# Weight sums, product order, bias and stores in a routed-LoRA FFN kernel

## The chip, the core and the metric

The kernel runs on one core of a Trainium2 chip. A core has TensorE (PE), VectorE (DVE), ScalarE (ACT), GpSimd (POOL) and SyncE (SP, which here only issues DMAs); each runs its own instructions in order, and they meet through semaphores. The metric is the device time of one execution in microseconds.

## The reference, cut to what matters

```python
z = einsum('bct,bcd->bdt', x, W[condition])        # 64 samples, 64x64 matrix for each, T = 1024
logits = einsum('bsd,ed->bse', z, gate_w)           # 8 experts, two are kept, softmax over the two
low    = einsum('bsd,erd->ebsr', z, lora_A)         # rank 16 for each expert
ffn    = z @ base_w.T + base_b + 2.0 * (low weighted by the gate) @ lora_B
out    = x + ffn
```

There are 64 x 64 = 4096 tokens of 1024 values, in fp32.

## The kernel before, in words

The per-sample 64x64 mix and the large product commute, so the kernel first multiplies x by all weights (lora_A, gate and base, 1160 columns) and then mixes tokens with a block-diagonal matrix (`bdr`, gathered for each tile by an indirect DMA on POOL). Every fp32 operand is split into a high part (a cast, mostly ACT, L199) and a low part (a subtraction, mostly DVE, L196), and each product is three matmuls: high x high, high x low, low x high.

The tokens are 32 tiles of 128. The 1160 columns are two halves of 580, each cut into chunks of 344 and 236 columns (`CS`), so that a tile has chunks c = 0 to 3. The contraction of 1024 is two halves of four k-blocks of 128. A product result goes to a PSUM bank z0 to z3; `split_z` splits it, and `sums` (L316) multiplies it by the block-diagonal matrix, adds the LoRA part, and leaves it in a bank a or o; `finish` (L334, DVE) adds that to the token tile `xtok`, which holds x and the bias; `store` (L339) writes the tile out. Chunk 0 also gives the gate (L344), whose small operations lead to a transpose (`tr`) and then to the LoRA matmuls.

Tiles 0 to 3 are done plainly (the first pair and the second, `plain`, L475). From tile 4 on, two tiles are taken as a 2x2 block product with seven products instead of eight (`pair`, L537): p1, p6, p2, p7, q4, q5, q3. Their weights are b11, b21 and b22, which are parts of the weight matrix, and t1 to t4, which are sums of parts; `sum_w` (L251) makes the sums in four rounds, each with four loads into the staging tiles `st`, four sums on DVE and four splits, while the second plain pair runs. The x operands are sums as well (`sum_x`, L230). The pairs use the staging tiles for their combinations u, v and w (L544 to L550).

The order of instructions on each engine is worked out by a list planner (`Program`, L55 to L134): each step has engines, an estimated cost, what it reads and writes, a due time and a lag, the time between a step's end and its result being there. A step goes to the engine that can begin first; at equal readiness the one with the earliest latest start goes first. Loads without inputs are held back until 10 us (`AHEAD`) before that. The real engines then run in that order and wait where the real times are longer. SP issues all plain loads and all stores; POOL issues the gathers and a few early splits.

Buffers that matter here: six raw x tiles (`xr`), three token tiles (tile i uses i % 3), four staging tiles, two block-diagonal tiles. Each token tile is loaded by `load_tok` (L268), and DVE adds the bias, which lies broadcast in `bias_bc`:

```python
add(SP, 1.45, lambda e: nc.sync.dma_start(xtok[j], x[i * P:(i + 1) * P, :]), ...)
add(DVE, 1.2, lambda e: nc.vector.tensor_tensor(xtok[j], xtok[j], bias_bc, ALU.add), ...)
```

Of the kernel before, what the change touches and what calls it, by code (L numbers as in the profile page):

```python
# [20 lines left out]
P = 128  # L21
# [22 lines left out]
SAME = {PE: 0.0, ACT: 0.1, DVE: 0.12, POOL: 0.1, SP: 1.0}  # L44
START = {PE: 0.0, ACT: 2.0, DVE: 0.8, POOL: 1.7, SP: 1.6}
GATHER = 8.0
AHEAD = 10.0
MARGIN = 1.2
COL = 0.0004557
LEAST = 0.107  # L50
PAIR = 28.6
LAG, LAST = 16.0, 8.0


# [83 lines left out]
def cond_ffn_kernel(ctx, tc, xT, x, idx, cw, wall, bias, lb, out):  # L138
# [15 lines left out]
    def many(n, shape, dt, name):  # L154
        return [sb.tile(shape, dt, name=f"{name}{j}") for j in range(n)]
# [4 lines left out]
    wl = {(m, s): sb.tile([P, KH, n], F32R, name=f"wl_{m}_{s}") for m in NAMES for s, n in enumerate(CS)}  # L160
    BLOCK = (("b11", "t4"), ("b21", "b22"))
    lbh, lbl = sb.tile([P, T], F32R, name="lbh"), sb.tile([P, T], F32R, name="lbl")
    bias_bc = sb.tile([P, T], F32, name="bias_bc")
    ident = sb.tile([P, P], F32, name="ident")
    NXR, NXA, NZ = 6, 4, 3
    xr, xtok = many(NXR, [P, KH, P], F32, "xr"), many(3, [P, T], F32, "xtok")
    xh, xl = many(NXA, [P, KH, P], F32R, "xh"), many(NXA, [P, KH, P], F32R, "xl")
    st = many(4, [P, 2 * CS[0]], F32, "st")
    bdr, bdh, bdl = many(2, [P, P], F32, "bdr"), many(2, [P, P], F32R, "bdh"), many(2, [P, P], F32R, "bdl")
    zh, zl = many(NZ, [P, CS[0]], F32R, "zh"), many(NZ, [P, CS[0]], F32R, "zl")  # L170
    low = many(2, [P, NG + 6], F32, "low")
# [23 lines left out]
    def sub(e, o, a, b):  # L195
        eng[e].tensor_tensor(o, a, b.bitcast(F32), ALU.subtract)  # L196
# [8 lines left out]
        return turns[kind] % n  # L205

    def tt_cost(n, e=DVE):
        return 0.08 + 0.00104 * n if e == DVE else 0.12 + 0.0022 * n


    def load_x(i, h, pieces=1):

        j, n = take("xr", NXR), KH // pieces
        for k in range(0, KH, n):
            add(SP, 0.182 * n, lambda e, k=k: nc.sync.dma_start(xr[j][:, k:k + n], xT[i][:, KH * h + k:KH * h + k + n]),  # L215
                writes=[("xr", j, q) for q in range(k, k + n)])
        return j

    def split_x(r, pieces=1, hi=ACT, lo=DVE):
# [10 lines left out]
    def sum_x(o, a, b, f):  # L230
        keys = lambda r: [("xr", r, q) for q in range(KH)]
        add(DVE, tt_cost(P * KH), lambda e: nc.vector.tensor_tensor(xr[o], xr[a], xr[b], f),  # L232
            [k for r in (a, b) if r != o for k in keys(r)], keys(o))


    def piece(j, s):
        return st[j][:, :2 * CS[s]].rearrange("p (k n) -> p k n", k=2)
# [5 lines left out]
    def split_w(j, m, s, k, hi=ACT, lo=DVE):  # L243
        n, a, q = 2 * CS[s], slice(k, k + 2), range(k, k + 2)
        src = [("st", j, 0), ("st", j, 1)]
        add(hi, 0.2 + (0.00083 if hi == ACT else 0.00052) * n, lambda e: copy(e, wh[m, s][:, a], piece(j, s)),
            src, [("wh", m, s, b) for b in q])
        add(lo, tt_cost(n, lo), lambda e: sub(e, wl[m, s][:, a], piece(j, s), wh[m, s][:, a]),
            src + [("wh", m, s, b) for b in q], [("wl", m, s, b) for b in q])

    def sum_w(s, k):  # L251
        keys = lambda j: [("st", j, 0), ("st", j, 1)]

        def plus(o, a, b):
            add(DVE, tt_cost(2 * CS[s]), lambda e: nc.vector.tensor_tensor(piece(o, s), piece(a, s), piece(b, s), ALU.add),  # L255
                keys(b if o == a else a), keys(o))
        for j, (h, n) in enumerate(((0, 0), (0, 1), (1, 1), (1, 0))):
            load_w(j, h, n, s, k)
        plus(0, 0, 1)
        split_w(0, "t1", s, k)  # L260
        plus(1, 1, 2)
        split_w(1, "t3", s, k)
        plus(0, 0, 2)
        split_w(0, "t2", s, k)
        plus(3, 3, 0)
        split_w(3, "t4", s, k)

    def load_tok(i):  # L268
        j = i % 3
        add(SP, 1.45, lambda e: nc.sync.dma_start(xtok[j], x[i * P:(i + 1) * P, :]),  # L270
            writes=[("xtok", j, c) for c in range(4)])
        add(DVE, 1.2, lambda e: nc.vector.tensor_tensor(xtok[j], xtok[j], bias_bc, ALU.add),  # L272
            ["bias"], [("xtok", j, c) for c in range(4)])

    def load_cond(i):

# [9 lines left out]
    due = {}  # L286

    def mm_cost(n):
        return max(COL * n, LEAST)

    def zstep(key, b, a, ka, m, s, start, stop):

# [45 lines left out]

    def store(i, cs):  # L339
        o, j = slice(outs(cs[0])[1].start, outs(cs[-1])[1].stop), i % 3  # L340
        add(SP, 0.00145 * (o.stop - o.start),
            lambda e: nc.sync.dma_start(out[i * P:(i + 1) * P, o], xtok[j][:, o]), [("xtok", j, c) for c in cs])

    def gate(i, b):  # L344

# [53 lines left out]

    ORDER = [(i, 0, k) for k in range(KT) for i in range(2)]  # L400
    ORDER += [(i, c, k) for i, c in ((0, 1), (1, 1), (0, 2), (0, 3), (1, 2), (1, 3)) for k in range(KT)]
    PRODUCTS = ("p1", "p6", "p2", "p7", "q4", "q5", "q3")
    t = 4.2
    for i, c, k in ORDER:
# [3 lines left out]
    for q in range(1, NPLAIN):  # L408
        for i in (2 * q, 2 * q + 1):
            for c in range(4):  # L410
                for k in range(KT):
                    due["plain", i, c, k] = t
                    t += 3 * mm_cost(CS[c % 2]) * 1.27
        ends.append(t)
    for q in range(NPLAIN, NPAIR):
        for p in PRODUCTS:
            for s in range(2):
                for k in range(KH):
                    due[q, p, s, k] = t
                    t += PAIR / 56 * 2 * CS[s] / HALF  # L420
        ends.append(t)
# [13 lines left out]
    def load_split_x(i, h, **engines):  # L435
        raw0[i, h] = load_x(i, h, 2)
        xa0[i, h] = split_x(raw0[i, h], 2, **engines)

    def first_loads():
        for h in range(2):  # L440
            for i in range(2):
                load_split_x(i, h, lo=POOL)
                load_split_w(h, 0, 0, 2 * i)
    first_loads()

# [15 lines left out]
    for s in range(2):  # L461
        for h in range(2):
            for k in range(0, KH, 2):
                load_split_w(h, 1, s, k)
    add(SP, 1.45, lambda e: nc.sync.dma_start(bias_bc, bias.broadcast_to([P, T])), writes=["bias"])
    load_tok(0)
    lraw = [("xtok", 2, c) for c in range(4)]
    add(SP, 1.45, lambda e: nc.sync.dma_start(xtok[2], lb), writes=lraw)
# [41 lines left out]
    def operands(q):  # L510

        a, b = 2 * q, 2 * q + 1
        a11 = load_x(a, 0)
        yield split_x(a11)
        a21, a22 = load_x(b, 0), load_x(b, 1)
        s3 = take("xr", NXR)
        sum_x(s3, a11, a21, ALU.subtract)
        sum_x(a21, a21, a22, ALU.subtract)
        sum_x(a11, a21, a11, ALU.subtract)
        yield split_x(a11)  # L520
        a12 = load_x(a, 1)
        yield split_x(a12)
        yield split_x(s3)
        yield split_x(a22)
        yield split_x(a21)
        sum_x(a12, a12, a11, ALU.add)
        yield split_x(a12)
# [9 lines left out]
    def pair(q):  # L537
        a, b = 2 * q, 2 * q + 1
        bx, by = (("z0", "z1"), ("z2", "z3"))[::1 if q % 2 else -1]
        u, v, w = q % 2, 2, 3  # L540
        part = lambda j, s: st[j][:, s * CS[0]:s * CS[0] + CS[s]]
        z = lambda bs, s: bank[bs[s]][:, :CS[s]]

        def combine(o, x, y, f, bs, reads=()):  # L544

            def then(s):
                at = {"o": part(o, s), "u": part(u, s), "v": part(v, s), "z": z(bs, s)}
                add(DVE, 0.09 + 0.00104 * CS[s], lambda e: nc.vector.tensor_tensor(at["o"], at[x], at[y], f),  # L548
                    [bs[s]] + [("st", j, s) for j in reads if j != o], [("st", o, s)])
            return then  # L550

        def chunk(i, n, o):
            return lambda s: post(i, 2 * n + s, split_z(CS[s], part(o, s), ("st", o, s), 0.05))

        ops = operands(q)
        product(q, "p1", next(ops), bx, True, False, lambda s: add(
            ACT, 0.2 + 0.00085 * CS[s], lambda e: copy(e, part(u, s), z(bx, s)), [bx[s]], [("st", u, s)]))
        product(q, "p6", next(ops), by, True, True, combine(u, "u", "z", ALU.add, by))
        product(q, "p2", next(ops), bx, False, True,
                lambda s: post(a, s, split_z(CS[s], z(bx, s), bx[s])))  # L560
        product(q, "p7", next(ops), by, True, False, combine(v, "u", "z", ALU.add, by, (u,)))

        def both(f, g):
            return lambda s: (f(s), g(s))
        product(q, "q4", next(ops), by, False, True,
                both(combine(w, "u", "z", ALU.add, by, (u,)), chunk(b, 0, w)))
        product(q, "q5", next(ops), bx, True, False,
                both(combine(v, "z", "v", ALU.subtract, bx), chunk(b, 1, v)))
        store(b, range(4))
        product(q, "q3", next(ops), bx, False, True,  # L570
                both(combine(u, "z", "u", ALU.subtract, bx), chunk(a, 1, u)))
        if q < NPAIR - 1:
            store(a, range(4))
        else:
            for cs in ((0, 1), (2,), (3,)):
                store(a, cs)
# [48 lines left out]
```

## Time and profile before

| | us |
|---|---|
| median of 3 runs | 507.07 (505.77 to 507.86) |
| the profiled execution | 507.96 |
| its span, first to last instruction | 506.1 |
| first matmul of the product / last matmul of all, start | 4.80 / 501.95 |
| mean granted TensorE clock | 0.990 |
| DMA share in 0-50 / 60-95 / 95-490 | 0.73 / 0.42 / 0.33 |

The page gives the busy time and share of each engine, then the span in 40 slices, the DMA queues, the chain of work that ended last, groups of instructions, and DMA issues. A group is named by line, engine, operation and out<-in tiles. A wait is given as "who <- whom: us in total, times, longest". In rows in order of time, the first number is the start and the second the duration, both in us; "[1.0 <-DVE st L548]" is idle time before it and what ended it. A line can be that of a helper: L196 is every subtraction of a split and L199 every cast.

### The profile page before, as it was taken

Reading aid. Unit: us, or ns where it says so; the run is one execution under the profiler, and the core shown is the slowest. Engines: PE = TensorE matmul, PEld = TensorE weight load, DVE = VectorE, ACT = ScalarE, POOL = GpSimd, SP = SyncE. Lnnn points to the kernel's source line nnn. Section 1 sums busy time; section 2 is a strip of 40 time slices with the busy share of each in tenths; the row PEclk is TensorE's granted clock in tenths of the full one; section 3 lists DMA queues with packets and bytes.
Section 4 is the critical chain, followed back from the end, with each engine's and each line's share of the span. In section 5 each row is a group of like instructions: output and inputs, shape, how many; then the busy total and the mean of one; then the engine's idle time right before and its main releaser. Section 6 shows DMA issues by size and latency. Waiting matters only on the chain.

```text
span 506.1 us, 9262 instructions
## 1 busy us (share of the span) xinstructions
PE 484.9 (96%) x3565; PEld 479.0 (95%) x3565; DVE 370.9 (73%) x959; ACT 175.3 (35%) x429; POOL 44.1 (9%) x49
## 2 busy tenths in 40 slices
PE   8999985999999999999999999999999999999996
PEld 7989975999999999999999998999999999999996
DVE  3768679786876858778686876858687686867765
ACT  6634335233332323333142332324242232423312
POOL 6310000010100001010010101001020100101000
PEclk8999999899999999999999999999999999999999
DMA  8884635142508043070704316061340606134042
GB/s 253 279 310 125 207 98 162 43 155 74 188 2 272 10 148 112 6 230 6 248 13 136 126 41 214 7 202 59 110 153 38 213 12 208 53 120 141 2 166 84
DMA packets 25292, 63.60 MB, mean 126 GB/s; under 512 B 3216, under 2 KB 6688, under 8 KB 25248
## 3 DMA queue, kind: packets, MB, share of 16 engines
q1 hardware_dynamic: 24192, 60.89, 35.7%
q0 software_dynamic: 1056, 2.12, 1.4%
q8 instruction: 28, 0.46, 0.4%
q14 instruction: 16, 0.13, 0.1%
HBM read 46.22 MB, written 16.78 MB: 124 GB/s over the span
## 4 chain that ended last, share of the span: by engine, by line
PE 73%; DMA 14%; DVE 8%; issue 1%; ACT 1%; SPq 1%; DVEq 0%; ACTq 0%
PE ps_z L298 56%; PE ps_o L329 12%; DMA xr<-in_xT 8%; DMA st<-in_w 6%; PE ps_a L329 4%; DVE st L255 1%; DVE wl_t L196 1%; DVE xl L196 1%; DVE xtok L336 1%; DVE wl_b L196 1%; DVE st L548 1%; DVE xr L232 1%; PE ps_a L372 1%; DVE zl L196 1%; SPq L215 1%
## 5 line engine op out<-in xcount | busy, mean ns | idle before, releaser
L298 PE MATMUL ps_z<-wh_t,xh 128*128 128x344 f32 x480 | 145.3, 303 | 9.3 <-DVE st L548 5.2
L298 PE MATMUL ps_z<-wl_t,xh 128*128 128x344 f32 x480 | 143.1, 298 | 1.0 <-DVE wl_t L196 1.0
L298 PE MATMUL ps_z<-wh_t,xl 128*128 128x344 f32 x480 | 142.8, 297 | 0.0
L298 PE MATMUL ps_z<-wh_b,xh 128*128 128x344 f32 (+1 forms) x432 | 131.9, 305 | 3.1 <-DVE zl L196 2.4
L298 PE MATMUL ps_z<-wl_b,xh 128*128 128x344 f32 (+1 forms) x432 | 130.3, 302 | 0.4 <-DVE wl_b L196 0.4
L298 PE MATMUL ps_z<-wh_b,xl 128*128 128x344 f32 (+1 forms) x432 | 129.8, 301 | 0.4 <-POOL xl L196 0.4
L298 PEld LDWEIGHTS ps_z<-wh_t,xh 128*128 128x128 f32 x480 | 91.1, 190 | 11.7 <-DVE st L548 6.9
L298 PEld LDWEIGHTS ps_z<-wl_t,xh 128*128 128x128 f32 x480 | 91.2, 190 | 1.5 <-DVE wl_t L196 1.5
L298 PEld LDWEIGHTS ps_z<-wh_t,xl 128*128 128x128 f32 x480 | 91.1, 190 | 0.0
L199 ACT CAST xh<-xr 128x512 fp32r<-128x512 f32 (+1 forms) x110 | 66.2, 605 | 70.2 <-PE ps_z L298 57.7
L298 PEld LDWEIGHTS ps_z<-wh_b,xh 128*128 128x128 f32 x432 | 83.2, 193 | 4.3 <-DVE zl L196 2.9
L298 PEld LDWEIGHTS ps_z<-wl_b,xh 128*128 128x128 f32 x432 | 83.2, 193 | 0.9 <-DVE wl_b L196 0.9
L298 PEld LDWEIGHTS ps_z<-wh_b,xl 128*128 128x128 f32 x432 | 83.1, 192 | 0.9 <-POOL xl L196 0.9
L196 DVE TENSOR_TENSOR xl<-xr,xh 128x512 fp32r<-128x512 f32 x102 | 69.8, 685 | 5.0 <-ACT xh L199 3.9
L278 POOL DMA_INDIRECT bdr<-in_cw,rows x32 | 33.7, 1053 | 414.2 <-DVE bdl L196 385.8
L199 ACT CAST zh<-st 128x344 fp32r<-128x344 f32 (+1 forms) x84 | 36.6, 436 | 83.7 <-DVE st L548 41.4
L336 DVE TENSOR_TENSOR xtok<-ps_o,xtok 128x344 f32<-128x344 f32 (+1 forms) x96 | 42.1, 439 | 32.0 <-PE ps_o L329 31.5
L232 DVE TENSOR_TENSOR xr<-xr,xr 128x512 f32<-128x512 f32 x56 | 38.5, 687 | 20.2 <-DMA xr<-in_xT 20.0
L548 DVE TENSOR_TENSOR st<-st,ps_z 128x344 f32<-128x344 f32 x84 | 37.6, 450 | 11.5 <-PE ps_z L298 11.3
L272 DVE TENSOR_TENSOR xtok<-xtok,bias_bc 128x1024 f32<-128x1024 f32 x32 | 38.8, 1214 | 7.9 <-DMA xtok<-in_x 7.9
L199 ACT CAST zh<-ps_z 128x344 fp32r<-128x344 f32 (+1 forms) x44 | 17.6, 400 | 69.7 <-PE ps_z L298 52.7
L196 DVE TENSOR_TENSOR zl<-st,zh 128x344 fp32r<-128x344 f32 (+1 forms) x84 | 37.9, 454 | 0.9
(68 smaller groups left out, 626.8 us busy)
## 6 DMA issues: line engine op xcount, KB each, us to landing
xtok<-in_x SPq DMA_DIRECT2D x32, 512.0 KB, 6.0
out<-xtok SPq DMA_DIRECT2D x31, 512.0 KB, 2.9
xr<-in_xT SPq DMA_DIRECT2D x60, 256.0 KB, 4.5
st<-in_w SPq DMA_DIRECT2D x16, 344.0 KB, 4.5
st<-in_w SPq DMA_DIRECT2D x16, 236.0 KB, 2.9
xr<-in_xT SPq DMA_DIRECT2D x8, 128.0 KB, 4.7
bdr<-in_cw,rows POOLq DMA_INDIRECT x32, 2.5
xtok<-in_lb SPq DMA_DIRECT2D x1, 512.0 KB, 5.7
```

The source lines that it names most:

```text
L196: eng[e].tensor_tensor(o, a, b.bitcast(F32), ALU.subtract)
L199: (nc.scalar.copy if e == ACT else nc.vector.tensor_copy)(o, a)
L215: add(SP, 0.182 * n, lambda e, k=k: nc.sync.dma_start(xr[j][:, k:k + n], xT[i][:, KH * h + k:KH * h + k + n]), writes=[("xr", j, q) for q ...
L232: add(DVE, tt_cost(P * KH), lambda e: nc.vector.tensor_tensor(xr[o], xr[a], xr[b], f), [k for r in (a, b) if r != o for k in keys(r)], key ...
L255: add(DVE, tt_cost(2 * CS[s]), lambda e: nc.vector.tensor_tensor(piece(o, s), piece(a, s), piece(b, s), ALU.add), keys(b if o == a else a) ...
L272: add(DVE, 1.2, lambda e: nc.vector.tensor_tensor(xtok[j], xtok[j], bias_bc, ALU.add), ["bias"], [("xtok", j, c) for c in range(4)])
L278: add(POOL, 1.04, lambda e: nc.gpsimd.indirect_dma_start(out=bdr[j], out_offset=None, in_=cw, in_offset=bass.IndirectOffsetOnAxis(ap=rows[ ...
L298: nc.tensor.matmul(z, l[a][:, ka, :], w[m, s][:, ka, :], start=(start and q == 0), stop=(stop and q == 2), skip_group_check=True)
L329: nc.tensor.matmul(d, l, r, start=(start and m == 0), stop=(stop and m == len(mms) - 1), skip_group_check=True)
L336: add(DVE, 0.09 + 0.00104 * (s.stop - s.start), lambda e: nc.vector.tensor_tensor(xtok[j][:, o], bank[b][:, s], xtok[j][:, o], ALU.add), [ ...
L372: add(PE, 0.107, lambda e: nc.tensor.matmul(tp, low[i % 2][:, :ER], ident, is_transpose=True, start=False, stop=False, skip_group_check=True),
L548: add(DVE, 0.09 + 0.00104 * CS[s], lambda e: nc.vector.tensor_tensor(at["o"], at[x], at[y], f), [bs[s]] + [("st", j, s) for j in reads if ...
```

## The change

- `sum_w`: the four sums are made first, in place (st0 = b00 + b01 for t1, st1 = st1 + st2 for t3, st2 = st2 + st0 for t2, st3 = st3 + st2 for t4); then the splits follow in the order t2, t3, t4, t1, and their low parts may go to DVE or POOL.
- The first pair (`NPLAIN`) runs its products in the order p1, p2, q3, p6, p7, q4, q5, with its own bank use, operand order and an additional staging tile; both stores come at its end.
- The bias tile goes. After the token load a DMA issued by POOL adds the bias, read broadcast from HBM, into the token tile.
- The stores of all but the last two tiles are issued by POOL.
- `xr` has seven buffers, `st` five. The low parts of the first x operand go to DVE instead of POOL.
- The planner gets lags for x loads (2.0), token loads (4.0), the accumulating DMA (5.0) and POOL's stores (2.0), and other costs for matmuls and POOL.

```diff
-COL = 0.0004557
-LEAST = 0.107
-PAIR = 28.6
+XLAG = 2.0
+COL, SET = 0.000418, 0.014
+LEAST = 0.111
+PAIR = 29.1
...
-    bias_bc = sb.tile([P, T], F32, name="bias_bc")
-    NXR, NXA, NZ = 6, 4, 3
+    NXR, NXA, NZ = 7, 4, 3
-    st = many(4, [P, 2 * CS[0]], F32, "st")
+    st = many(5, [P, 2 * CS[0]], F32, "st")
...
-        return 0.08 + 0.00104 * n if e == DVE else 0.12 + 0.0022 * n
+        return 0.08 + 0.00104 * n if e == DVE else 0.15 + 0.0035 * n
...
-                writes=[("xr", j, q) for q in range(k, k + n)])
+                writes=[("xr", j, q) for q in range(k, k + n)], lag=XLAG if pieces == 1 else 0.0)
...
         plus(0, 0, 1)
-        split_w(0, "t1", s, k)
         plus(1, 1, 2)
-        split_w(1, "t3", s, k)
-        plus(0, 0, 2)
-        split_w(0, "t2", s, k)
-        plus(3, 3, 0)
-        split_w(3, "t4", s, k)
+        plus(2, 2, 0)
+        plus(3, 3, 2)
+        for j, m in ((2, "t2"), (1, "t3"), (3, "t4"), (0, "t1")):
+            split_w(j, m, s, k, lo=(DVE, POOL))
...
-        add(SP, 1.45, lambda e: nc.sync.dma_start(xtok[j], x[i * P:(i + 1) * P, :]),
-            writes=[("xtok", j, c) for c in range(4)])
-        add(DVE, 1.2, lambda e: nc.vector.tensor_tensor(xtok[j], xtok[j], bias_bc, ALU.add),
-            ["bias"], [("xtok", j, c) for c in range(4)])
+        keys = [("xtok", j, c) for c in range(4)]
+        add(SP, 1.45, lambda e: nc.sync.dma_start(xtok[j], x[i * P:(i + 1) * P, :]), writes=keys, lag=4.0)
+        add(POOL, 1.1, lambda e: nc.gpsimd.dma_start(xtok[j], bias.broadcast_to([P, T]), accum_op=ALU.add),
+            writes=keys, lag=5.0)
...
-        return max(COL * n, LEAST)
+        return max(COL * n + SET, LEAST)
...
-        add(SP, 0.00145 * (o.stop - o.start),
-            lambda e: nc.sync.dma_start(out[i * P:(i + 1) * P, o], xtok[j][:, o]), [("xtok", j, c) for c in cs])
+        src = [("xtok", j, c) for c in cs]
+        if i < NT - 2:
+            add(POOL, 1.0, lambda e: nc.gpsimd.dma_start(out[i * P:(i + 1) * P, o], xtok[j][:, o]), src, lag=2.0)
+        else:
+            add(SP, 0.5, lambda e: nc.sync.dma_start(out[i * P:(i + 1) * P, o], xtok[j][:, o]), src)
...
+    FIRST = ("p1", "p2", "q3", "p6", "p7", "q4", "q5")
...
-                    t += 3 * mm_cost(CS[c % 2]) * 1.27
+                    t += 3 * mm_cost(CS[c % 2]) * 1.25
-        for p in PRODUCTS:
+        for p in FIRST if q == NPLAIN else PRODUCTS:
...
-                load_split_x(i, h, lo=POOL)
+                load_split_x(i, h, lo=POOL if h or i else DVE)
...
-    add(SP, 1.45, lambda e: nc.sync.dma_start(bias_bc, bias.broadcast_to([P, T])), writes=["bias"])
...
         yield split_x(a11)
+        if q == NPLAIN:
+            a12 = load_x(a, 1)
+            yield split_x(a12)
...
+        if q == NPLAIN:
+            sum_x(a12, a12, a11, ALU.add)
+            for r in (a12, a11, s3, a22, a21):
+                yield split_x(r)
+            return
...
-        u, v, w = q % 2, 2, 3
+        u, v, w = 4 if q == NPLAIN else q % 2, 2, 3
...
+        if q == NPLAIN:
+
+            t = 1
+            product(q, "p2", next(ops), bx, False, True,
+                    lambda s: post(a, s, split_z(CS[s], z(bx, s), bx[s])))
+            product(q, "q3", next(ops), by, True, True, lambda s: None)
+            product(q, "p6", next(ops), bx, True, True,
+                    both(combine(u, "u", "z", ALU.add, bx), combine(t, "y", "u", ALU.subtract, by, (u,))))
+            product(q, "p7", next(ops), bx, True, False, combine(v, "u", "z", ALU.add, bx, (u,)))
+            product(q, "q4", next(ops), bx, False, True,
+                    both(combine(w, "u", "z", ALU.add, bx, (u,)), chunk(b, 0, w)))
+            product(q, "q5", next(ops), by, True, True,
+                    both(both(combine(v, "z", "v", ALU.subtract, by), chunk(b, 1, v)),
+                         both(combine(t, "z", "t", ALU.add, by), chunk(a, 1, t))))
+            store(b, range(4))
+            store(a, range(4))
+            return
```

More of the change, by code (lines that the diff above doesn't have):

```diff
@@ L247, in split_w @@
             src, [("wh", m, s, b) for b in q])
-        add(lo, tt_cost(n, lo), lambda e: sub(e, wl[m, s][:, a], piece(j, s), wh[m, s][:, a]),
+        lo = lo if isinstance(lo, tuple) else (lo,)
+        add(lo, [tt_cost(n, e) for e in lo], lambda e: sub(e, wl[m, s][:, a], piece(j, s), wh[m, s][:, a]),
             src + [("wh", m, s, b) for b in q], [("wl", m, s, b) for b in q])
@@ L255, in plus @@
             add(DVE, tt_cost(2 * CS[s]), lambda e: nc.vector.tensor_tensor(piece(o, s), piece(a, s), piece(b, s), ALU.add),
-                keys(b if o == a else a), keys(o))
+                [q for j in (a, b) if j != o for q in keys(j)], keys(o))
         for j, (h, n) in enumerate(((0, 0), (0, 1), (1, 1), (1, 0))):
@@ L546, in then @@
             def then(s):
-                at = {"o": part(o, s), "u": part(u, s), "v": part(v, s), "z": z(bs, s)}
+                at = {"o": part(o, s), "u": part(u, s), "v": part(v, s), "t": part(1, s), "z": z(bs, s)}
+                at["y"] = at["z"]
                 add(DVE, 0.09 + 0.00104 * CS[s], lambda e: nc.vector.tensor_tensor(at["o"], at[x], at[y], f),
@@ L553, in chunk, with both @@
             return lambda s: post(i, 2 * n + s, split_z(CS[s], part(o, s), ("st", o, s), 0.05))
+        def both(f, g):
+            return lambda s: (f(s), g(s))
         ops = operands(q)
@@ L561, in pair @@
         product(q, "p7", next(ops), by, True, False, combine(v, "u", "z", ALU.add, by, (u,)))
-        def both(f, g):
-            return lambda s: (f(s), g(s))
         product(q, "q4", next(ops), by, False, True,
```

## The prediction

> **What bounds the kernel now.** I read the page's busy times first, then stretches of the span, then the matmul rows, and only then asked who is waited for. TensorE is busy or queued nearly always:
>
> ```profile
> PE 484.9 (96%) x3565; PEld 479.0 (95%) x3565; DVE 370.9 (73%) x959; ACT 175.3 (35%) x429; POOL 44.1 (9%) x49
> ...
> PEclk8999999899999999999999999999999999999999
> ```
>
> In the rows in order of time, back-to-back matmuls start 0.1575 us apart at 344 columns, 0.1115 at 236 and 0.107 at 208, so the matmul work has a price that no edit here changes. A plain tile is 8 x 3 x 2 x (0.1575 + 0.1115) = 12.9 us, a pair's seven products 7 x 12 x 0.269 = 22.6; the sums of one tile are 3.2. Four plain tiles (64.4) and 14 pairs (29.0 each, 405.4) make 469.8. The first real matmul starts at 4.80 and the last at 501.95: 497.2 us, so **27.3 us are lost**. Adding up, row by row, what each start is later than its spacing gives 6.5 us lost in 0-50, 0.0 in 50-60, 11.4 in 60-95, 8.4 in 95-490 and 1.1 after. The stretches (length, then busy time and instructions of each engine, granted clock, DMA) show the same place:
>
> ```profile
> 50.00:60.00 10.00, 10.00 (x74) 10.00 (x73) 7.10 (x16) 3.50 (x8) 0.94 (x1) 1.00 0.64 199
> 60.00:95.00 35.00, 27.27 (x182) 26.45 (x181) 26.02 (x57) 13.21 (x28) 1.15 (x1) 0.90 0.42 133
> 95.00:490.00 395.00, 389.85 (x2911) 387.73 (x2910) 295.69 (x789) 130.83 (x333) 27.33 (x26) 1.00 0.33 111
> ```
>
> So there are two things to gain: a bad 35 us while the weight sums are made, and a small repeated loss in the pairs. In the first, three stalls carry it: 1.7 us at 62.87, 2.0 at 74.62, and 7.5 from 82.49 to 92. The third, in TensorE's rows:
>
> ```profile
> 82.49 0.27 PE L298 MATMUL ps_z<-wh_t,xl 128*128 128x236 f32 x1
> 86.67 0.57 PE L298 MATMUL ps_z<-wh_t,xh 128*128 128x236 f32 x1 [3.91 <-ACT wh_t L199]
> 87.73 0.57 PE L298 MATMUL ps_z<-wl_t,xh 128*128 128x236 f32 x1 [0.49 <-DVE wl_t L196]
> 88.09 0.42 PE L298 MATMUL ps_z<-wh_t,xl 128*128 128x236 f32 x1
> ```
>
> The second product (p6, weight t2) reaches a part of t2 that isn't made yet. After the wait the matmuls are longer (0.42 for 0.27), and until 92.1 they start 0.12 to 0.13 us late each: the granted clock has fallen (0.81 in 80-90). VectorE's rows show why the first stall is there: it stood 3.2 us in front of a bias addition, with a gate's work behind it.
>
> ```profile
> 61.45 1.23 DVE L272 TENSOR_TENSOR xtok<-xtok,bias_bc 128x1024 f32<-128x1024 f32 x1 [3.22 <-DMA xtok<-in_x]
> 62.59 0.16 DVE L362 SCALAR_TENSOR_TENSOR wf<-l,e 128x8 f32<-128x8 f32 x1
> ```
>
> In the pairs, the waits and SyncE's queue:
>
> ```profile
> PE ps_z L298 <- DVE st L548: 5.2, 8, 1.7
> ...
> SPq L342 <- DVE xtok L336: 341.3, 31, 24.4
> ```
>
> ```profile
> 183.08 0.34 SPq L342 DMA_DIRECT2D out<-xtok  x1
> 183.52 1.15 SPq L215 DMA_DIRECT2D xr<-in_xT  x2
> 185.70 0.34 SPq L342 DMA_DIRECT2D out<-xtok  x1
> 186.10 0.42 SPq L215 DMA_DIRECT2D xr<-in_xT  x1
> ```
>
> SyncE stands in front of stores, and loads of x are queued behind. The chain of waits runs through such a load: issued at 183.52, landed near 189.3, VectorE waiting 2.33 us for it, TensorE stopped 1.7. Eight such stalls are worth 6.4 of the 8.4 us.
>
> **Part by part.** Sums run against the profiled execution's own 507.96 us (span 506.1, 1.9 around it); the median shown, 507.07, lies 0.9 below that.
>
> *Bias off VectorE.* 32 additions of 1.21 us (38.8) go, and the waits in front of them (7.9 over four). Most lay beside matmuls, as VectorE is 73% busy; on the path is the gate's stall: -1.6, a gate's remaining operations needing some 0.7 us. What is late next is the load of x that landed at 62.7, which TensorE needs only from 76.7. The one bias load on SP (0.42 us to issue) goes too.
>
> *The new wait.* A tile's token buffer now passes through: store issued by POOL (0.95, the gather's row, the nearest POOL DMA), landing 2.9, token load issued 0.42 and landing 6.0, accumulation issued 0.95 and landing unknown. The nearest row for the last is the broadcast bias load, 7.4 us, which moves the same bytes from the same place: sum 18.6. Today the first tile's last finish of a pair ends at 245.09 and the first finish on the same buffer (three buffers, second tile of the next pair) starts at 268.62: 23.5 us, less 0.5 as pairs get shorter. Slack is 4.4 us, so I cost it at nothing. The Trainium skill, "DMA: Bandwidth & Descriptors", section on the anatomy of a GpSimd-issued DMA, gives 2.0 us + bytes/436e3, an estimate of 3.2 us and a slack of 8.6; the row is longer, and I take the row. No run here shows an accumulation: the other end is twice the row (its destination is read as well), 14.8, late by 3.0 us. Behind a finish that waits, all of VectorE's queue stands: combines, splits, then TensorE.
>
> *Stores by POOL.* The same page, section "Issuing engines are not separate DMA queues", speaks against this: spreading DMAs saves only the sequencer's issue time. Thirty stores at 0.34 us on a queue that is mostly idle are then worth nothing, and the sum below would end at 499.7 instead of 494.5. The row says something else: what costs is SP's wait *in front of* a store, 341 us, with x loads behind. By the row the eight stalls go; I leave 0.15 us on each: -5.2. The page is right about bandwidth (DMA share 0.33 in the pairs), not about a queue's order. Next late is a load behind a token load that waits for the longer store; the x loads' added planned 2.0 us and the seventh xr buffer cover a few us of it. POOL has two gathers, two accumulations and two stores a pair, about 6 of 29 us; a gather queued behind a store has a tile's time to land.
>
> *Sums ahead of splits, three products without sums first.* Sums and splits stay 16 each (0.865/0.645 and 0.869/0.642 us on VectorE). In a round four sums run first, so the last round's t2 would come no sooner after its loads (83.2 + four sums 2.3 + split = 86.7, as today). The gain is in the need: p2 and q3 come before p6, two products of 3.2 us. Today p6's late part is asked for at 82.6; with 2.6 us of the earlier stalls gone (below) and 6.4 of product added, at about 86.4. Against that, the round starts earlier: its loads waited for staging buffers behind VectorE's stalled queue (3.2 us bias wait, 4 additions of 1.2). So t2 is ready near 82 and the whole third stall goes, the clock's share with it: -7.2 of 7.5. POOL may take low-part splits: 1.0 us for 256 elements, so some 2.7 for 688, beside other work; if it stretches VectorE's rows (one 688 split is 1.38 instead of 0.87 beside POOL at 11.3), it's tenths. The second stall is a zl behind a sum that waited 1.1 us for weights; weight loads get no longer planned landing, so I count half: -1.0, and +0.8 for further sums that wait ahead of splits.
>
> *New tight places in the first pair.* p1->p2, p6->p7 (two combines, 0.5 us each, in one bank) and q5->next p1 reuse a bank after only 1.34 us (one 236-column half). ACT or VectorE fits by tenths or not: bounds 0 and 2.5, taken +1.2.
>
> *The rest.* First x split on VectorE instead of POOL (0.35 for 1.1 us, but behind a 0.88 split): 0 to -1.5, taken -0.5. Planner numbers move order only: nothing. The tail's stores stay on SP: nothing.
>
> Sum: -1.6 - 1.0 - 7.2 + 0.8 + 1.2 - 0.5 - 5.2 = **-13.5**; 494.5 by this execution, **493.6** as a median.
>
> **Rivals.**
> - *Late bias (slower).* One mechanism: accumulations land after VectorE's first finish on the buffer. VectorE stands, TensorE runs on about 1 us (less than one half-product, 1.34) and then stops. It decides from 7.4 + 4.4 + 1 + 13.5/14 = 13.8 us of landing. At 14.8, VectorE stands 3.0 us a pair and TensorE loses 2.0, x 14 = 28: near 522. For it: nothing measured, and the reads of one HBM row by 128 partitions are already slow (7.4 against 6.0). Against: 4.4 us of slack, DMA share 0.33. 6%.
> - *Weight stage still late.* t2 arrives 4 us after need, half the stall stays: near 497.8. For: in-order engines wait for weight loads planned too short. 18%.
> - *Stores don't matter.* x loads now wait behind token loads: the pairs keep their 8.4 us, 498.8. 11%.
> - *All of it.* Both losses vanish: 508.0 - 11.4 - 7.0 - 1.0 - 0.9 = 487.7. 7%.
> - *Forecast*, 490 to 497: 58%.
>
> A measurement tells about 0.5% (2.5 us) from no change. Faster 0.92, same 0.03, slower 0.05. The range 489 to 500 holds the forecast, both partial cases and the upper part of the last.
>
> **What would show it.** Right: no wait near 4 us before the pairs, clock 1.0 in 80-95, first pair's t2 split ended before its product; SP's wait for VectorE gone, x loads landing ahead of their sums; eight stalls down to tenths. Wrong: VectorE idle in front of a finish until an accumulation lands (late bias); TensorE still waiting for wh_t or wl_t; a new PE wait on ACT's copy or on combines over 0.5 us.

## The result, and the profile after

The changed kernel takes 503.08 us (median of 7 runs, 500.14 to 504.58); in the same comparison the kernel before takes 507.88. The ratio is 0.9908, 95% interval 0.988 to 0.9936. It is faster, but by 4.8 us where 13.5 were forecast, and its time lies above the forecast range of 489 to 500. The profiled execution took 503.61 us with a span of 501.8 (before: 507.96 and 506.1).

First two rows of the page, then the stretches of the span (length, busy time and instructions of PE, PEld, DVE, ACT and POOL, granted clock, DMA share, GB/s):

```profile
PE 484.2 (96%) x3565; PEld 479.9 (96%) x3565; DVE 343.4 (68%) x924; ACT 174.0 (35%) x429; POOL 100.9 (20%) x116
...
PEclk8988999989999999999999999999999999999999
```

```profile
0.00:50.00 50.00, 41.84 (x266) 39.34 (x267) 30.98 (x61) 23.52 (x48) 17.95 (x22) 0.90 0.78 238
50.00:60.00 10.00, 9.52 (x72) 9.07 (x71) 8.49 (x14) 3.80 (x8) 4.99 (x4) 1.00 0.38 133
60.00:95.00 35.00, 31.79 (x236) 31.13 (x235) 22.17 (x54) 10.97 (x27) 6.77 (x7) 1.00 0.61 173
```

In 60-95 TensorE now does 236 matmuls, 182 before: the bad stretch is better. But the clock row (40 slices of 12.5 us) has two new 8s between 25 and 50 us, and in 0-50 only 266 matmuls were done, at a mean clock of 0.90; before, it was 318 at 0.97. Adding up by how much each matmul starts later than its spacing, as the prediction did, gives the account. The last column is the median of each kernel's runs; the others come from one profiled execution, which lay up to 2.8 us from that median (a_oldsum).

| kernel (those below are explained in the next section) | first matmul at | lost 0-50 | 50-130 | 130-480 | after 480 | median |
|---|---|---|---|---|---|---|
| before | 4.80 | 6.5 | 12.2 | 7.5 | 1.1 | 507.9 |
| changed | 6.04 | 11.9 | 8.8 | 0.9 | 0.1 | 503.1 |
| b_store | 4.97 | 6.3 | 10.3 | 0.9 | 1.1 | 499.2 |
| b_xlag | 4.85 | 6.2 | 10.7 | 0.5 | 0.7 | 498.2 |
| b_xw | 4.83 | 7.4 | 8.8 | 0.8 | 0.8 | 498.3 |
| b_xacc | 4.86 | 8.0 | 10.4 | 0.8 | 0.8 | 499.4 |
| a_spstore | 7.01 | 10.5 | 12.1 | 1.4 | 0.8 | 507.2 |
| after_nopool | 5.95 | 9.6 | 7.1 | 0.9 | 0.1 | 499.7 |
| after_emit | 5.98 | 11.5 | 5.7 | 0.9 | 0.1 | 500.1 |
| a_lb | 6.86 | 7.0 | 11.3 | 0.9 | 0.1 | 503.2 |
| a_oldpair | 6.51 | 10.0 | 13.0 | 0.8 | 0.8 | 507.2 |
| a_nopool | 6.71 | 9.9 | 3.2 | 1.1 | 0.8 | 497.8 |
| a_oldsum | 6.13 | 10.9 | 9.1 | 1.1 | 0.1 | 500.6 |
| a_wlag | 6.36 | 10.4 | 1.6 | 1.1 | 0.8 | 495.2 |
| a_best | 7.32 | 4.4 | 1.8 | 1.0 | 0.8 | 490.8 |
| a_bestpool | 5.78 | 4.6 | 4.6 | 1.3 | 0.7 | 493.7 |
| a_bestsp | 6.02 | 5.7 | 2.1 | 1.2 | 0.7 | 491.1 |

From before to changed: start +1.2 + 5.4, weight stage -3.4, pairs -6.6, end -1.0, together -4.4 against 4.3 of span. So the pairs gave more than forecast, the weight stage less than half, and the start lost 6.6 where 0.5 were to be won. The late first matmul has no part in that loss, since TensorE waits less just after it: counted from the first, the 101st matmul starts at 21.74 us (21.82 before), the 131st at 26.27 (26.85 before), but the 201st at 44.63 (37.42 before).

**The new loss at the start.** TensorE's and then ScalarE's rows of the changed kernel, in order of time:

```profile
31.21 0.32 PE L297 MATMUL ps_z<-wh_t,xl 128*128 128x344 f32 x1
34.51 0.43 PE L328 MATMUL ps_a<-zh,bdh 128*128 128x344 f32 x1 [2.98 <-ACT bdh L199]
```

```profile
33.21 1.06 ACT L472 ACTIVATE lbh<-xtok 128x1024 fp32r<-128x1024 f32 x1 [4.96 <-DMA xtok<-in_lb]
34.17 0.28 ACT L199 CAST bdh<-bdr 128x128 fp32r<-128x128 f32 x1
```

The cast of the second block-diagonal tile takes 0.28 us and its data is long there; it stands behind the scaling of lora_B, which waited 4.96 us for its load. SyncE's rows tell why: the load is issued at 24.43, behind a token load at 16.99; before (second block), it was issued at 17.07 and the token loads after it.

```profile
16.99 1.51 SPq L270 DMA_DIRECT2D xtok<-in_x  x1
...
24.43 0.42 SPq L470 DMA_DIRECT2D xtok<-in_lb  x1
```

```profile
17.07 0.58 SPq L468 DMA_DIRECT2D xtok<-in_lb  x1
```

The new lags (4.0 on the token load, 5.0 on the accumulation behind it) make a token load look urgent; lora_B's load got none. (No run leaves these two lags out; the planner's order, worked out from its code, has lora_B's load in front again without the 5.0.) After the stall the matmuls of 344 columns start 0.29 us apart instead of 0.1575, until 41.4 us; the granted clock was 0.56 in 34-41.5.

**The weight stage.** VectorE's rows, and POOL's in the same time:

```profile
39.57 2.00 DVE L196 TENSOR_TENSOR xl<-xr,xh 128x512 fp32r<-128x512 f32 x1
...
44.83 2.38 DVE L256 TENSOR_TENSOR st<-st,st 128x688 f32<-128x688 f32 x1
```

```profile
39.27 1.75 POOL L196 TENSOR_TENSOR wl_t<-st,wh_t 128x688 fp32r<-128x688 f32 x1 [3.61 <-ACT wh_t L199]
44.64 1.83 POOL L196 TENSOR_TENSOR wl_t<-st,wh_t 128x688 fp32r<-128x688 f32 x1 [3.61 <-ACT wh_t L199]
```

An xl of this size usually takes 0.69 us, and such a sum 0.88. Each ends some 0.55 to 0.75 us after the POOL split beside it (41.57 after 41.02; 47.21 after 46.47), as if it had begun only then. Seven low-part splits of the weight sums ran on POOL (the expectations below say nine), and all seven do this, 6.8 us of VectorE time in all.

The accumulations are late once, for tile 2 (first row). Its token load was issued at 49.00; the accumulation was issued by POOL at 61.32 (second row), after two splits and two stores in POOL's queue, and took 10.9 us to land, the longest of the 32. And p6 no longer waits for t2 but for its bank (TensorE's rows, then VectorE's):

```profile
72.36 0.82 DVE L335 TENSOR_TENSOR xtok<-ps_o,xtok 128x236 f32<-128x236 f32 x2 [4.25 <-DMA xtok<-in_bias]
```

```profile
61.32 0.97 POOL L271 DMA_DIRECT2D xtok<-in_bias  x1
```

```profile
96.94 0.27 PE L297 MATMUL ps_z<-wh_b,xl 128*128 128x236 f32 x1
99.00 0.42 PE L297 MATMUL ps_z<-wh_t,xh 128*128 128x344 f32 x1 [1.79 <-DVE zl L196]
```

```profile
94.20 0.65 DVE L256 TENSOR_TENSOR st<-st,st 128x472 f32<-128x472 f32 x1 [1.42 <-DMA st<-in_w]
...
97.88 0.65 DVE L196 TENSOR_TENSOR wl_t<-st,wh_t 128x472 fp32r<-128x472 f32 x1
98.44 0.51 DVE L196 TENSOR_TENSOR zl<-ps_z,zh 128x344 fp32r<-128x344 f32 x1
```

The split that frees p2's bank stands in VectorE's queue behind the last round's sums and splits. That round runs from 94.2; before it ran from 83.3. It is late because its loads are: SyncE stood 14.0 us in front of a load into a staging tile until VectorE had split the first round's t4 out of it, and the last seven weight loads went out only after that. Before, the same load went out at 68.91 (last row).

```profile
78.37 0.88 DVE L196 TENSOR_TENSOR wl_t<-st,wh_t 128x688 fp32r<-128x688 f32 x1 [0.20 <-ACT wh_t L199]
79.27 13.31 SPq L240 DMA_DIRECT2D st<-in_w  x7
```

```profile
68.91 4.18 SPq L240 DMA_DIRECT2D st<-in_w  x2
```

**The pairs.** No wait over 0.2 us is left in TensorE's rows from 130 to 480. VectorE's waits for x loads in that stretch, before, were those of the first row; in the changed kernel there are none. SP's waits (the other two rows) are of another kind:

```profile
DVE xr L232 <- DMA xr<-in_xT: 18.9, 14, 2.6
```

```profile
SPq L270 <- DMA out<-xtok: 260.2, 14, 23.5
SPq L215 <- DVE xr L232: 84.0, 14, 12.0
```

SP stands in front of a token load until a store has landed; the x loads are queued behind it and still arrive in time.

### The profile page after: what moved, and what is told of

The parts are those of the page before. It is cut to its first block, busy times and chain, and to the rows that moved or that the text cites. A ratio compares the mean times of both kernels' runs of the same rounds, so it can differ in the third digit from the quotient of the medians.

```text
span 501.8 us, 9370 instructions
## 1 busy us (share of the span) xinstructions
PE 484.2 (96%) x3565; PEld 479.9 (96%) x3565; DVE 343.4 (68%) x924; ACT 174.0 (35%) x429; POOL 100.9 (20%) x116
## 4 chain that ended last, share of the span: by engine, by line
PE 83%; DMA 8%; DVE 4%; issue 2%; ACT 1%; SPq 1%; POOL 0%; DVEq 0%; ACTq 0%
PE ps_z L297 64%; PE ps_o L328 13%; PE ps_a L328 5%; DMA st<-in_w 5%; DMA xtok<-in_bias 2%; DMA xtok<-in_lb 2%; DVE st L256 1%; DVE wl_b L196 1%; PE ps_a L374 1%; DVE xtok L335 1%; DVE zl L196 1%; SPq L215 1%; DVE wl_t L196 0%; ACT wh_t L199 0%; SPq L240 0%
## 5 line engine op out<-in xcount | busy, mean ns | idle before, releaser
L196 DVE TENSOR_TENSOR xl<-xr,xh 128x512 fp32r<-128x512 f32 (+1 forms) x104 | 74.8, 720 | 29.6 <-ACT xh L199 27.9
L342 POOL DMA_DIRECT2D out<-xtok x30 | 17.2, 574 | 227.7 <-DVE xtok L335 227.7
L271 POOL DMA_DIRECT2D xtok<-in_bias x32 | 29.6, 926 | 114.7 <-DMA xtok<-in_x 113.8
L277 POOL DMA_INDIRECT bdr<-in_cw,rows x32 | 34.8, 1086 | 11.2 <-issue 4.6
```

Source lines behind the costliest of these rows:

```text
L271: add(POOL, 1.1, lambda e: nc.gpsimd.dma_start(xtok[j], bias.broadcast_to([P, T]), accum_op=ALU.add), writes=keys, lag=5.0)
L277: add(POOL, 1.04, lambda e: nc.gpsimd.indirect_dma_start(out=bdr[j], out_offset=None, in_=cw, in_offset=bass.IndirectOffsetOnAxis(ap=rows[ ...
L342: add(POOL, 1.0, lambda e: nc.gpsimd.dma_start(out[i * P:(i + 1) * P, o], xtok[j][:, o]), src, lag=2.0)
```

## The experiments

Each kernel was timed beside the kernel before; its median in these four comparisons was 505.6, 507.4, 506.4 and 507.1 us. Kernels of different comparisons are therefore better compared by their ratios: a difference of 0.002 in the ratio is 1 us. Not tried alone: the seventh x buffer, the fifth staging tile, the new costs for matmuls and POOL, and the lags of token loads and accumulations.

**Which edit cured the pairs?** Three kernels. b_store takes only the stores' part of the change into the kernel before:

```diff
-        add(SP, 0.00145 * (o.stop - o.start), ...)
+        if i < NT - 2:
+            add(POOL, 1.0, lambda e: nc.gpsimd.dma_start(...), src, lag=2.0)
+        else:
+            add(SP, 0.5, lambda e: nc.sync.dma_start(...), src)
```

> The kernel before, with only the stores of all but the last two tiles issued by POOL. Theory A (x loads were late because they stood behind stores in SP's queue): the eight stalls of 0.3 to 1.7 us in the pairs go, the loss in 95-490 falls from 8.4 to 2 us or less, 501 to 503. Theory B (the planner's 2.0 us lag on x loads did it, or the bias off VectorE): 506 to 508.

b_xlag takes only the planner's lag of x loads:

```diff
-                writes=[("xr", j, q) for q in range(k, k + n)])
+                writes=[("xr", j, q) for q in range(k, k + n)], lag=2.0 if pieces == 1 else 0.0)
```

> The kernel before, with only the lag of 2.0 us on x loads. Theory A (stores in SP's queue are the cause): loads are planned earlier but still stand behind stores, 505 to 508. Theory B (the plan was the cause): 501 to 503.

a_spstore is the changed kernel with `store` as it was before.

> The changed kernel with the stores back on SP, nothing else. Theory A: SP waits for VectorE in front of stores again, the pairs' loss returns from under 2 to about 8 us, 507 to 509. Theory B (lag or VectorE's relief did it): 502 to 504.

b_store took 499.23 us, ratio 0.9872 (0.9834 to 0.991); b_xlag 498.17, 0.9849 (0.9811 to 0.9888); a_spstore 507.18, 1.0014 (0.9987 to 1.0042). Both single edits cure the pairs (0.9 and 0.5 us lost in 130-480, before 7.5), and each alone gives at least as much as the whole change (ratio 0.9908, 0.988 to 0.9936). b_store came out below its 501 to 503, and b_xlag went against what I expected: SP still stands in front of stores (22.4 us at the longest), but the first x load of the next pair is now planned ahead of them.

```profile
150.47 0.33 SPq L215 DMA_DIRECT2D xr<-in_xT  x1
152.20 0.34 SPq L342 DMA_DIRECT2D out<-xtok  x1
152.60 0.42 SPq L215 DMA_DIRECT2D xr<-in_xT  x1
```

And a_spstore, though back at 507, isn't slow in the pairs (1.4 us lost): its loss is in the first 130 us, where another order came out. That its time lies in the range of Theory A is luck. So "x loads are late because stores stand ahead of them" holds, but the changed kernel has two cures for it, and the stores' move is not needed beside the other.

**Is lora_B's load the start's loss?** a_lb is the changed kernel with one number:

```diff
-    add(SP, 1.45, lambda e: nc.sync.dma_start(xtok[2], lb), writes=lraw)
+    add(SP, 1.45, lambda e: nc.sync.dma_start(xtok[2], lb), writes=lraw, lag=2.0)
```

> The changed kernel, with one planner number more: the load of lora_B gets a lag of 2.0, which puts it back ahead of the first token load. Theory A (the new token lags pulled token loads ahead of lora_B; ScalarE then stood 5.0 us in front of its scaling, with a block-diagonal cast behind it): both stalls at 27 and 31 us and the half clock after them go, the loss in 0-50 falls from 11.9 to about 6.5 us, tile 2's finish no longer waits 4.3 us for its bias, and the time is 496 to 498.5. Theory B (the start is slower because accumulations and token loads take DMA time from weights): another load is late in its place, 501 to 503.

503.24 us, ratio 0.9953 (0.9936 to 0.9971): no gain, and above the ranges of both theories. The mechanism was right: the stalls at 27 and 31 us and the low clock are gone, tile 2's finish no longer waits for its accumulation, and the 201st matmul starts at 37.35, as before the change. The size was not: 50-130 loses 11.3 instead of 8.8, for TensorE now waits for VectorE. The longest such wait, 2.6 us at 84.8, is for the second of these rows, which stands behind a sum that waited for its weights:

```profile
83.07 0.88 DVE L256 TENSOR_TENSOR st<-st,st 128x688 f32<-128x688 f32 x1 [4.65 <-DMA st<-in_w]
...
84.47 0.28 DVE L196 TENSOR_TENSOR ltl<-ps_a,lth 128x128 fp32r<-128x128 f32 x1
```

**Do POOL's splits cost time?** a_nopool is a_lb, after_nopool the changed kernel, both with

```diff
-            split_w(j, m, s, k, lo=(DVE, POOL))
+            split_w(j, m, s, k)
```

> a_lb with all low parts of the weight-sum splits on VectorE (none on POOL). Theory C (a POOL split stops the VectorE operation beside it: xl took 2.0 to 2.2 us there instead of 0.69, a sum 2.4 instead of 0.88): no VectorE row is stretched, the loss in 50-110 falls from 12 to 9 or 10 us, 500 to 501.5. Rival (VectorE is late because it waits for loads, not because of POOL; the nine splits come back to it at 0.64 to 0.87 us each): 502.5 to 504.5.

> The changed kernel with all low parts of the weight-sum splits on VectorE, nothing else. Theory C (POOL's splits stretch VectorE's work and so delay finishes, staging tiles and loads): no stretched VectorE rows, the loss in 50-130 falls from 8.8 to 4 us or less while 0-50 stays near 11, 497 to 499.5. Rival (the splits on POOL only hurt together with the order that the lora_B lag gave): 501.5 to 504.

a_nopool took 497.79 us, ratio 0.9804 (0.9756 to 0.9852), after_nopool 499.74, 0.9843 (0.9783 to 0.9903): the medians are 5.4 and 3.3 us below the kernels with POOL's splits (by the ratios 7.6 and 3.3). a_nopool is thus faster than forecast, after_nopool slightly slower. In after_nopool the loss in 50-130 fell to 7.1 only, as a gate's transpose waits 3.2 us behind sums that wait for weights. But the planner had also chosen another order. after_emit keeps the order of every engine; the seven instructions that ran on POOL stand at the same places in VectorE's queue:

```diff
-        add(lo, [tt_cost(n, e) for e in lo], lambda e: sub(e, wl[m, s][:, a], ...), ...)
+        add(lo, [tt_cost(n, e) for e in lo], lambda e: sub(DVE, wl[m, s][:, a], ...), ...)
```

> The changed kernel with the same order on every engine, only that the nine splits that ran on POOL are issued to VectorE at the same places of the program. Theory C (stretching and slow splits on POOL cost time by themselves): VectorE gains the 6.3 us of stretch and pays 9 x 0.76 = 6.9 us, but no weight waits 1.7 us for POOL; 500 to 501.5. Rival (it was the planner's new order in after_nopool): 502.5 to 504.5, as the changed kernel.

500.08 us, ratio 0.9855 (0.9827 to 0.9883), as Theory C had it: 3.0 below the changed kernel's median, 2.7 by the ratios; the loss in 50-130 falls from 8.8 to 5.7 while the start keeps its 11.5. The xl that took 2.00 us is whole again, behind the split that POOL had:

```profile
39.06 0.88 DVE L196 TENSOR_TENSOR wl_t<-st,wh_t 128x688 fp32r<-128x688 f32 x1
...
40.40 0.68 DVE L196 TENSOR_TENSOR xl<-xr,xh 128x512 fp32r<-128x512 f32 x1
```

So giving splits to POOL cost time by itself, apart from the order. Whether the stretch of VectorE or the weight's later arrival (1.7 us on POOL for 0.88) costs more, this doesn't separate.

**Are sums and product order worth anything?** a_oldpair is a_lb with the first pair in the old order; a_oldsum is a_nopool with each sum followed by its split:

```diff
         plus(0, 0, 1)
+        split_w(0, "t1", s, k)
         plus(1, 1, 2)
-        plus(2, 2, 0)
-        plus(3, 3, 2)
-        for j, m in ((2, "t2"), (1, "t3"), (3, "t4"), (0, "t1")):
-            split_w(j, m, s, k)
+        split_w(1, "t3", s, k)
+        plus(0, 0, 2)
+        split_w(0, "t2", s, k)
+        plus(3, 3, 0)
+        split_w(3, "t4", s, k)
```

> a_lb with the first seven-product pair in the order of the kernel before (p1, p6, p2, p7, q4, q5, q3); sums stay in place ahead of splits. Theory E (the new order postpones t2's need by 6.4 us, and that is its gain): TensorE waits 4 us or more for wh_t or wl_t again, 506 to 509. Rival (the order gains nothing, as the last round is itself later than before and p6 then waits for its bank): 502 to 504.

> a_nopool with each sum followed by its split, in the order t1, t3, t2, t4 of the kernel before; product order new. If four sums ahead of the splits matter by themselves: slower than a_nopool by 1.5 us or more, 499.5 to 502. If only the product order does: 496.5 to 499.

a_oldpair took 507.2 us, ratio 0.9992 (0.9948 to 1.0035), 4.0 more than a_lb (2.0 by the ratios, whose intervals overlap), and TensorE waits for t2 again:

```profile
PE ps_z L297 <- ACT wh_t L199: 4.0, 1, 4.0
```

a_oldsum took 500.58, 0.9858 (0.9796 to 0.9919), 2.8 more than a_nopool; these intervals overlap too. So the new product order does take away the wait for t2, and both parts point to a gain of some 2 to 4 us; its size isn't shown, as a_oldpair also lost 3.0 us more than a_lb in 0-50, where another order came out.

**Do the sums wait for weights planned too early?** a_wlag is a_nopool, and b_xw is b_xlag, with

```diff
-            load_w(j, h, n, s, k)
+            load_w(j, h, n, s, k, 2.0)      # as lag of the load
```

> a_nopool with a planned lag of 2.0 us on the loads of the weight sums. Theory D (VectorE stands in front of sums whose weights were planned 2 to 3 us too early, 2.3 us at 58 and 4.7 us at 83 in a_lb): these waits shrink to under 1 us each, the stalls behind them (56, 82, 87) go, 497 to 499.5. Rival (staging tiles are held too long, so loads are late whatever is planned): within 1 us of a_nopool.

> b_xlag with a planned lag of 2.0 us on the loads of the weight sums; order of sums, products, bias and stores as before. Theory D: the 5.3 us wait for wh_t before p6 and the clock behind it shrink, 493 to 496. Rival (the rounds are bound by the staging tiles): 497 to 499.

a_wlag: 495.19 us, ratio 0.9759 (0.971 to 0.9809). From 50 to 110 us VectorE waits 0.7 us for weights, in a_nopool 6.4, and the loss in 50-130 falls from 3.2 to 1.6. The medians, taken side by side, differ by 2.6 us, but the intervals overlap. b_xw: 498.3, 0.9816 (0.9769 to 0.9863), no change against b_xlag that is clear of the noise: the wait for t2 fell from 5.3 to 4.5 us only. My reading, not shown, is that with the old order p6 asks for t2 before any planning can have it. What was left in a_wlag was one stall of 4.5 us at 38, behind the first round's weights:

```profile
38.35 0.88 DVE L256 TENSOR_TENSOR st<-st,st 128x688 f32<-128x688 f32 x1 [3.42 <-DMA st<-in_w]
...
41.71 0.88 DVE L256 TENSOR_TENSOR st<-st,st 128x688 f32<-128x688 f32 x1 [2.41 <-DMA st<-in_w]
42.51 0.34 DVE L367 SCALAR_TENSOR_TENSOR low<-low,r,wf 128x128 f32<-128x128 f32 x1
```

A gate's operations stand between two sums that wait. So a_best plans that round with 6.0:

```diff
-            load_w(j, h, n, s, k, 2.0)
+            load_w(j, h, n, s, k, 2.0 if s or k else 6.0)
```

> a_wlag with a planned lag of 6.0 us instead of 2.0 on the first round's weight loads, which land late while the start's loads are still moving. If VectorE's wait for that round (3.4 us at 38, in front of a gate) is what leaves 4.5 us at 38.2: that stall goes, the loss in 0-50 falls from 10.5 to 6, 490 to 492.5. Otherwise 494.5 to 496.5.

490.84 us (489.43 to 491.47), ratio 0.9664 (0.9604 to 0.9723). This is the best version found, 15.5 us below the kernel before, and inside the range expected for a cure of that stall; 0-50 loses 4.4. TensorE's longest wait is the one for its first product:

```profile
PE ps_z L297 <- ACT xh L199: 3.0, 1, 3.0
```

**What is worth keeping in it?** a_bestpool lets the splits go to POOL again, a_bestsp puts the stores back on SP:

> a_best with the low parts of the weight-sum splits free to go to POOL again. Theory C: VectorE rows stretched to about 2 us beside them, 492.5 to 495. Rival (with weight loads planned rightly there is room, and POOL's help costs nothing): 490 to 492.

> a_best with the stores back on SP. If the lag alone keeps x loads ahead (as in b_xlag): 490 to 493, pairs' loss under 2 us. If POOL's stores are needed: 8 us more in the pairs, 497 or over.

a_bestpool: 493.69 us (493.12 to 495.42), 0.9747 (0.9711 to 0.9783), 2.9 more than a_best and 2.6 more than a_bestsp, which was timed beside it and has no such splits on POOL. a_bestsp: 491.06, 0.9682 (0.9649 to 0.9715), the same as a_best.

**The bias alone.** b_xacc is b_xlag with the accumulating DMA instead of VectorE's addition, a lag of 4.0 on the token load and one of 2.0 on lora_B's load, which keeps its place (these two are left out here):

```diff
-        add(DVE, 1.2, lambda e: nc.vector.tensor_tensor(xtok[j], xtok[j], bias_bc, ALU.add), ...)
+        add(POOL, 1.1, lambda e: nc.gpsimd.dma_start(xtok[j], bias.broadcast_to([P, T]), accum_op=ALU.add),
+            writes=keys, lag=5.0)
```

> b_xlag with the bias by accumulating DMA (bias tile and its load gone, lora_B's load with a lag of 2.0 so that it keeps its place); sums, products and stores as before. If the bias on VectorE cost the path only the gate's stall: 496 to 498, and no finish waits for an accumulation in the pairs. If the longer way of a token tile (store, load, accumulation) decides: VectorE waits for accumulations, over 500.

499.42 us, 0.984 (0.9782 to 0.9899), between the two expectations: no finish waits for an accumulation, and there is nothing to gain either; the pairs stay at 0.8 and 0-50 loses 8.0 instead of 6.2.

## Why the prediction was wrong, step by step

The account of the profiled execution is 9.1 us short of the forecast (-4.4 for -13.5). The start misses by 7.1 and the weight stage by 4.4; the pairs and the end, better than forecast, give 2.4 back.

- **Pairs (-5.2): the cause right, its cure only half seen.** Late x loads were the cause, and the loss fell by 6.6 us. (The load of the prediction's example landed at 188.6, its neighbour at 189.3; this changes nothing.) But "planner numbers move order only: nothing" was wrong: the lag on x loads alone does it. The rival "stores don't matter" was wrong as it was put (x loads are not late behind token loads), and yet the move is worth nothing beside the lag (a_bestsp).
- **Start (-0.5, measured +6.6): the step that failed most is "Planner numbers move order only: nothing".** The term for the first x split did no harm: at the 131st matmul the changed kernel is 0.6 us ahead. The loss lies between 27 and 41.4 us and comes from the order: for engines that run in order, order *is* time. Lora_B's load was pushed back by 7.4 us behind a token load, and with it ScalarE, a stall of 3.0 us and slow matmuls; a_lb, which moves that load alone, takes all this away. The prediction had priced every instruction, but not the loads that a new lag overtakes. What a_lb showed besides: mending this stall alone gives nothing while VectorE is the next queue.
- **Weight stage (-7.8 with the bias, measured -3.4).** t2's wait went, as forecast, and its clock share with it (1.00 in 80-95). Three terms were mis-sized. "If it stretches VectorE's rows, it's tenths": it is 1.0 to 1.5 us for each of the four POOL splits of 688 and 0.3 to 1.0 for the three of 472, and some 3 us of the kernel's time (after_emit); a split of 688 itself took POOL 1.7 us, less than the 2.7 estimated. "The round starts earlier, t2 is ready near 82": the last round's sums began at 94.2, 10.9 us later than before, as its loads waited for a staging tile. And of the new tight places (+1.2), the one that cost was not among those named: p2's bank, which p6 takes over after a whole product in between. TensorE lost 1.9 us there, and the granted clock was 0.79 in 95-103.
- **Bias off VectorE (-1.6).** The gate's stall of 1.5 us at 62 is gone, but a finish stood 4.25 us for tile 2's accumulation, and TensorE lost 2.0 of it. In the pairs (130-480) an accumulation lands in 5.6 us (median), less than the 7.4 that I took, and none is waited for: the slower rival didn't come.

The gains that were forecast do exist. With lora_B's load in its place, no splits on POOL and lags on the weight loads, a_best is 15.5 us faster than the kernel before, more than the 13.5 forecast; but it took numbers that the change didn't have.

The prediction's view of the Trainium skill on issuing engines ("DMA: Bandwidth & Descriptors", "Issuing engines are not separate DMA queues") holds in part: moving the stores alone gave 6.4 us (b_store), as it frees a queue; with loads planned ahead of the stores it is worth nothing (a_bestsp), as the page would have it. For POOL's splits the page "SBUF — State Buffer", section "Who interferes with whom", would have been the one to weigh: it says that a VectorE instruction with two SBUF inputs contends with a GpSimd instruction that reads SBUF, over the port pair that the two share, which it calls an exclusive lock. The rows agree: 2.00 us for 0.69, ending right after POOL's.

## What to carry to other kernels

Where a planner writes the order, its numbers are part of the change: look for every load that a new lag overtakes, and for every wait that one optimistic landing puts into an in-order queue. A second engine for elementwise work isn't free help if it stops the first one; look at the rows of both in the same microseconds. And when several edits aim at one stall, try each alone: here one number (2.0 us on x loads) gave at least as much as the whole change, and five changed lines on top of the change gave 12 us.

## What was not expected of the hardware

- Beside a POOL tensor operation with two SBUF inputs, even a tiny VectorE operation was held up: in a_bestpool an 8-element subtraction with a per-partition operand took 1.46 us (median 0.22), ending when POOL's split of 2.23 us did:

```profile
52.81 1.46 DVE L361 TENSOR_SCALAR d<-low,mx 128x8 f32<-128x8 f32 x1
```

```profile
52.01 2.23 POOL L196 TENSOR_TENSOR wl_t<-st,wh_t 128x688 fp32r<-128x688 f32 x1 [1.10 <-ACT wh_t L199]
```

- A 512 KB store occupies POOL for 0.57 us, an accumulating DMA of the same size 0.92; an accumulation lands in 5.8 us (median; 4.9 to 10.9), no later than the 6.0 of a plain token load before the change.
